# One addition into interleaved chunks of z, and more column levels tied behind the joins, in a four-layer convolution kernel

## The chip, the cores and the metric

The kernel runs on one core of a Trainium2 chip. The metric is the device time of one execution in microseconds (us). Times below are medians of several runs, or come from one profiled execution where that is said. The engines are named as in the profile: PE (matrix products; PEld is its weight load), DVE (VectorE), ACT (ScalarE), POOL (GpSimd), and SP, which issues most of the transfers (DMA). SBUF is the on-chip memory the engines work in; PSUM is the memory PE writes its products to.

## The reference

Four layers act in turn on x of 4 images x 64 channels x 256 x 256 pixels, in float32. Layers 0, 1 and 3 convolve every channel with a separable filter (made by a small sine network), which the kernel does as two products with Toeplitz matrices per channel, and add a multiple of the input. Layer 2 is the one that the change touches. It transforms each image to Haar coefficients in both directions, mixes the channels at every coefficient in two ways, shrinks and sums the two, and transforms back:

```python
f1 = haar2d(x)
acc = jnp.zeros_like(f1[:, :conv_w.shape[1]])
for i in range(v.shape[0]):          # two terms
    f3 = f1 * v[i]
    f4 = jnp.einsum('bchw,oc->bohw', f3, conv_w[i])
    f5 = jnp.sign(f4) * jax.nn.relu(jnp.abs(f4) - tau[i])
    acc = acc + f5
y = haar2d(acc, inverse=True)
return y + x
```

## The kernel before

The four images go through three kinds of stage. `convolutions(b)` does layers 0 and 1 and the forward Haar transform of image b, channel by channel, and stores coefficients in DRAM. `mixing(b)` does the channel mixing and the shrinking, in 64 groups g of four coefficient rows (two stored rows, 2g and 2g+1). `inverse(b)` does the inverse Haar transform and layer 3, channel by channel, for 64 channels. The convolutions of image b+1 run beside the mixing of image b, and their last part beside its inverse. Of images 0 to 2 some channels skip layer 3 at first (`put_off`), are stored (`late`), and are done in `convolution` beside the mixing of image 3.

The order of the work is written as events: each step has a time in ticks (`at`, `PLACE`), and the events are emitted in that order. The framework's planner then places the instructions on each engine's queue when the kernel is built; it may take an instruction ahead of its written tick, as long as its inputs and its explicit ties allow. What counts is the order in the trace.

The tile z (32,768 floats in each of 128 partitions) holds the mixed coefficients of one image. Its free dimensions before are n, s, x, c: n is the chunk (channels 16n to 16n+15), s the slot of a stored row (`slot(i)`, 128 of them), x the four pieces of a row, c the channel in the chunk.

In mixing, for each group: `mix` makes the products on PE; `scaled` (DVE, L502) and `scaled_too` (ACT, L507) multiply them by coefficients into f4, of 16 pieces of 64 channels. `N_ACT` says how many of the 16 pieces ACT takes: 12 for images 0 to 2, 8 for image 3. So DVE takes 4 pieces in one instruction, and for image 3 it takes 8 in two. `size` and `sign` are on ACT (L511, L514), `shrink` and `signed` on DVE (L518, L522). `add` (L528) sums the two terms into z, one DVE instruction for each of the group's two rows, 256 elements each. The output channels come in the order of the columns of `wmix`, n then c, and `add` writes them in runs of 16.

The column direction of the inverse transform is done on z itself. `level(n, chunk, begin, count)` does one step of it for one chunk of 16 channels: `halve` subtracts (L326) and then forms the other half by `scalar_tensor_tensor` (L329), in place, over n rows (or `count` of them) of 64 contiguous elements. Chunk 0 is not done in this way: its 16 channels go through PE instead (`halves`, `cols`). For chunks 1 to 3 there are levels n = 1, 2, 4, 8 and 16 in one piece each, n = 32 in two pieces of 16 rows and n = 64 in four. `butterfly` does a first small step for all chunks. A level of n rows needs the rows that the first 2n slots bring, so it may run while mixing still goes on.

In inverse, `fetch` (ACT, L569) copies one channel out of z, 512 elements that lie 64 floats apart for s and 16 for x; `rows` transforms them on PE; `join` (DVE, L598, L601, L602) adds the rest and makes u, from which layer 3 starts on PE (`contract`, L286 and L287; a copy on ACT, L300; the sum on DVE, L317). Channel c is fetched at tick `start + c + 0.414`, so chunk 1 is first wanted at tick 16, chunk 2 at 32 and chunk 3 at 48 of the stage.

`LATE[b]` lists pieces (chunk, n, i) of the levels that are held back: each is cut into two halves of 8 rows, placed at the two ticks given, and tied behind the join emitted last before it (`stay=True`, `behind[0]`, "not ahead of the joins"). Pieces that are not in the list are not tied.

Of the kernel before, what the change touches and what calls it, by code (L numbers as in the profile page):

```python
# [9 lines left out]
F32 = mybir.dt.float32  # L10
F32R = mybir.dt.float32r
AF = mybir.ActivationFunctionType
ALU = mybir.AluOpType
# [3 lines left out]
B, C, S, EMB, ORD = 4, 64, 256, 33, 64  # L17
P = 128
# [63 lines left out]
    "l add": 3.47,  # L82
}

LATE = (
    {
        (2, 64, 3): (21, 23),
        (3, 32, 0): (18, 19),
        (3, 32, 1): (25, 27),
# [2 lines left out]
        (3, 64, 2): (34, 35),  # L92
        (3, 64, 3): (37, 38),
    },
    {(2, 64, 3): (21, 23), (3, 64, 1): (24, 26), (3, 64, 2): (28, 31), (3, 64, 3): (34, 37)},
    {(2, 64, 3): (21, 23), (3, 64, 1): (24, 26), (3, 64, 2): (28, 31), (3, 64, 3): (34, 37)},
    {},
)

# [11 lines left out]
def conv_seq_kernel(ctx, tc, x, fz, fw, bias, decay, haar, haar_row, factors, vt, taut, wmix, out):  # L111
# [14 lines left out]
    nc = tc.nc  # L126
# [5 lines left out]
    zpool = ctx.enter_context(tc.tile_pool(name="zpool", bufs=1))  # L132
# [13 lines left out]
    bsb = const.tile([P, 3, C], F32, name="bsb")  # L146


    z = zpool.tile([P, 4, P, 4, 16], F32, name="z")

    sd = zpool.tile([P, 8, 2, 2, P], F32, name="sd")
    sums = zpool.tile([P, 4, 2, P], F32, name="sums")
# [6 lines left out]

    room = z.rearrange("p n s x c -> p (n s x c)")
    free = [0]

    def part(n, parts=P):
# [158 lines left out]
    def halve(even, odd, stay=False):  # L324

        first = nc.vector.tensor_sub(odd, even, odd)  # L326
        if stay and behind[0] is not None:
            tc.add_manual_dep(first.ins, behind[0].ins.name, order, reason="not ahead of the joins")
        nc.vector.scalar_tensor_tensor(even, even, 2.0, odd, ALU.mult, ALU.subtract)  # L329

    def level(n, chunk, begin=0, count=None, stay=False):

        count = n if count is None else count
        v = z.rearrange("p n s x c -> p n s (x c)")[:, chunk].rearrange("p (j e s) x -> p j e s x", e=2, s=P // 2 // n)
        halve(v[:, begin : begin + count, 0, 0, :], v[:, begin : begin + count, 1, 0, :], stay)

    def butterfly():

        v = z.rearrange("p n s (k h) c -> p n s k h c", k=2)
        for h in range(2):  # L340
            halve(v[:, :, 0, 0, h, :], v[:, :, 0, 1, h, :])

# [3 lines left out]
    def at(time, run, unit):  # L348
        events.append((time, len(events), run, unit))
# [104 lines left out]
    def mixing(b, start, n_act):  # L454

        st = {}

        def load(g):
            f = mx.tile([P, 2, S], F32, name=f"f_{b}_{g}", tag="f", bufs=3)
            nc.sync.dma_start(f, coef[b].rearrange("k c p w -> (k c) p w")[:, 2 * g : 2 * g + 2])  # L460
            st[g] = {"f": f}
            if g % GT == 0:
                t = mx.tile([P, 2, GT, 16], F32, name=f"vt_{b}_{g}", tag="vt")
                nc.sync.dma_start(t, scales[:, g // GT])
                st["vt", g // GT] = t

        def scale(g, i):
            return st["vt", g // GT][:, i, g % GT, :]

        def over(g, i, n):  # L470
            return scale(g, i)[:, :n].unsqueeze(2).to_broadcast([P, n, C])

        def mix(g):
            f = st[g]["f"]
            ps = psx.tile([P, 2, 2, S], F32, name=f"px_{b}_{g}", tag="mix")
            for q in range(2):
                for h in range(2):
                    for r in range(2):
                        half = slice(r * C, (r + 1) * C)
                        nc.tensor.matmul(  # L480
                            ps[:, r, q, h * P : (h + 1) * P],
                            f[half, q, h * P : (h + 1) * P],
                            wb[half],
                            start=True,
                            stop=True,
                        )
            if g == 0:

                one, two = ps[:, 0, 0], ps[:, 1, 0]
                d = mx.tile([P, S], F32, name=f"d_{b}", tag="mag")  # L490
                nc.vector.tensor_copy(d, two)
                nc.vector.tensor_sub(two, one, d)
                nc.vector.tensor_add(one, one, d)
            st[g]["f4"] = mx.tile([P, 16, C], F32, name=f"f4_{b}_{g}", tag="f4")
            st[g]["px"] = ps.rearrange("p r q (h i o) -> p r q (h i) o", h=2, i=2)

        def scaled(g):
            px, n = st[g]["px"], 16 - n_act
            for r in range(n // 4):
                j = slice(4 * r, 4 * r + 4)  # L500
                v = scale(g, 0)[:, j].unsqueeze(2).to_broadcast([P, 4, C])
                nc.vector.tensor_tensor(st[g]["f4"][:, j], px[:, r, 0], v, ALU.mult)  # L502

        def scaled_too(g, half):
            px, f4 = st[g]["px"], st[g]["f4"]
            for j in range(16 - n_act + half * (n_act // 2), 16 - (1 - half) * (n_act - n_act // 2)):
                nc.scalar.mul(f4[:, j], px[:, j // 4 % 2, j // 8, j % 4], scale(g, 0)[:, j : j + 1])  # L507

        def size(g):
            mag = st[g]["mag"] = mx.tile([P, 16, C], F32, name=f"mag_{b}_{g}", tag="mag")  # L510
            nc.scalar.activation(mag, st[g]["f4"], AF.Abs)  # L511

        def sign(g):
            nc.scalar.activation(st[g]["f4"], st[g]["f4"], AF.Sign)  # L514

        def shrink(g):
            mag = st[g]["mag"]
            nc.vector.tensor_sub(mag, mag, over(g, 1, 16))  # L518

        def signed(g):  # L520
            mag = st[g]["mag"]
            nc.vector.scalar_tensor_tensor(mag, mag, 0.0, st[g]["f4"], ALU.max, ALU.mult)  # L522

        def add(g):
            parts = st.pop(g)["mag"].rearrange("p (q x i) (n c) -> p q i x n c", q=2, i=2, n=4)
            for q in range(2):
                to = slot(2 * g + q)
                nc.vector.tensor_add(  # L528
                    z[:, :, to].rearrange("p n x c -> p x n c"), parts[:, q, 0], parts[:, q, 1]
                )  # L530


        for g in range(S // 4):
            for name, stage in zip(
                ("mix load", "mix", "scaled", "scaled too", "scaled rest", "size", "sign", "shrink", "signed", "add"),
                (
                    load,
                    mix,
                    scaled,
                    lambda g: scaled_too(g, 0),  # L540
                    lambda g: scaled_too(g, 1),
                    size,
                    sign,
                    shrink,
                    signed,
                    add,
                ),
            ):
                at(start + g + PLACE[name if b + 1 < B else "l " + name], stage, g)

    def inverse(b, start, put_off):

        st = {}
# [11 lines left out]

        def fetch(c):
            a = mx.tile([P, 2, 2, P], F32, name=f"zc_{b}_{c}", tag="mag")
            v = z[:, c // 16, :, :, c % 16].rearrange("p i (k h) -> p h k i", k=2)
            nc.scalar.copy(a, v)  # L569
            st[c]["z"] = a  # L570

# [38 lines left out]
        def when(tick, n, chunk, *span, stay=False):  # L610
            at(tick + PLACE["level"], lambda _: level(n, chunk, *span, stay=stay), 0)

        at(along + 11 + PLACE["level"], lambda _: butterfly(), 0)
        for chunk in range(1, 4):
            turn = start + 16 * (chunk - 1)
            for n in (1, 2, 4, 8):
                when(along + 12 + 3 * chunk if b + 1 < B else turn, n, chunk)
            if chunk == 3 and b + 1 < B:
                turn = start + 15
            when(turn + 1, 16, chunk)  # L620
            for n in (32, 64):
                for i in range(n // 16):
                    tick = LATE[b].get((chunk, n, i))
                    if tick is None:
                        when(turn + n // 16 + (n == 64) * 2 + 2 * i, n, chunk, 16 * i, 16)
                    else:
                        for j in range(2):
                            when(start + tick[j], n, chunk, 16 * i + 8 * j, 8, stay=True)

        for c in range(C):  # L630
            for name, stage in zip(("sooner", "early", "fetch", "rows"), (sooner, early, fetch, rows)):
                at(start + c + PLACE[name], stage, c)
            turn = start + c
# [75 lines left out]
    start = ready + 3  # L709
    for b in range(B):  # L710
# [10 lines left out]
        start = max(end + C, ready + 3)  # L721
# [5 lines left out]
def slot(i):  # L727

    if i == 0:
        return 0  # L730
    n = 1 << i.bit_length() - 1
    return (2 * (i - n) + 1) * (P // 2 // n)
# [104 lines left out]
```

## Time and profile before

| what | value |
|---|---|
| median of 3 runs | 2844.78 us (2844.46 to 2845.08) |
| the profiled execution, in the same measure | 2842.56 us |
| its span in the profile | 2840.7 us |
| PE busy | 2732.7 us, 96% |
| DVE busy | 2494.6 us, 88% |
| ACT busy | 2077.6 us, 73% |
| POOL busy | 333.9 us, 12% |
| first to last start of `add` (L528), image 0 | 448.7 to 846.9 us |
| the same, images 1, 2, 3 | 1051.8 to 1483.4, 1694.8 to 2126.4, 2332.5 to 2607.7 us |
| first to last start of `fetch` (L569), image 0 | 848.0 to 1029.6 us |
| the same, images 1 and 3 | 1483.8 to 1672.7, 2608.3 to 2823.8 us |
| granted PE clock | full speed throughout |

The span is what the profile records from its first to its last event; the time of the execution has 1.9 us around it. Busy time is the time in which at least one instruction of the engine was under way. Instructions of one engine overlap a little: the mean duration of one is somewhat longer than the distance from its start to the start of the next. A tick is no fixed time: in image 0, the 64 channels of the inverse take 182 us, about 2.9 us each.

### The profile page before, as it was taken

To read this page: it belongs to the slowest core of one execution; us is meant where nothing else is said; L and a number is where in the kernel's file an instruction comes from. 1 tells how busy PE (TensorE), PEld (TensorE's weight loads), DVE (VectorE), ACT (ScalarE), POOL (GpSimd) and SP (SyncE) were. 2 spreads that over 40 slices of the span, in tenths; PEclk is the share of its full clock that TensorE was granted. 3 is DMA by queue.
4 is the path that set the end of the run, shared out by engine and by line. 5 is a ranking of instruction groups with operands and counts; after the bars stand their busy time and mean duration, and the time that the engine had idled before them with its cause. 6 is when DMAs were issued, how large, how long until landed. Compare 5 with 4: busy or idle time off the path is not lost. (4 is left out here: it accounts for less than half of the span.)

```text
span 2840.7 us, 56683 instructions
## 1 busy us (share of the span) xinstructions
PE 2732.7 (96%) x18642; PEld 2438.6 (86%) x18642; DVE 2494.6 (88%) x4333; ACT 2077.6 (73%) x4941; POOL 333.9 (12%) x644
## 2 busy tenths in 40 slices
PE   9999999999999999999999999999999999899999
PEld 8999998888889898888889998888889987787998
DVE  5655558999998979999998879999998889999985
ACT  2333348999986559989886658999985669998554
POOL 0111111121111001212210001312210000000000
PEclk9999999999999999999999999999999999999999
DMA  6877787676667886777677986777778988787786
GB/s 200 258 232 231 227 239 220 209 208 208 206 207 251 287 257 203 211 212 209 205 216 246 292 262 201 210 210 214 208 212 241 296 277 249 234 253 228 227 240 200
DMA packets 597209, 653.20 MB, mean 230 GB/s; under 512 B 44625, under 2 KB 513204, under 8 KB 596660
## 3 DMA queue, kind: packets, MB, share of 16 engines
q1 hardware_dynamic: 545460, 599.82, 70.6%
q10 hardware_dynamic: 51456, 49.75, 5.1%
q8 instruction: 150, 2.46, 0.4%
q14 instruction: 143, 1.17, 0.1%
HBM read 428.34 MB, written 221.05 MB: 229 GB/s over the span
## 5 line engine op out<-in xcount | busy, mean ns | idle before, releaser
L286 PE MATMUL py<-t,a 128*128 128x256 f32 x3072 | 946.3, 390 | 48.7 <-ACT a L300 47.7
L300 ACT COPY a<-pa 128x512 f32<-128x512 f32 x768 | 475.1, 619 | 476.6 <-PE pa L287 448.3
L507 ACT ACTIVATE f<-px,vt 128x64 f32<-128x64 f32 x2816 | 607.6, 354 | 104.2 <-DVE f L502 101.9
L287 PEld LDWEIGHTS py<-t,a 128*128 128x128 f32 x3072 | 583.4, 190 | 79.3
L287 PE MATMUL py<-t,a 128*128 128x128 f32 x3072 | 590.0, 274 | 0.0
L286 PEld LDWEIGHTS py<-t,a 128*128 128x128 f32 x3072 | 479.4, 191 | 112.2 <-ACT a L300 74.6
L380 POOL TENSOR_TENSOR sd<-less 128x128 f32<-128x128 f32 (+4 forms) x320 | 188.5, 589 | 1829.7 <-DVE less L379 1498.1
L286 PE MATMUL pa<-t,y 128*128 128x256 f32 x1024 | 316.5, 391 | 45.0 <-DVE y L317 44.2
L569 ACT COPY zc<-z 128x512 f32<-128x512 f32 x256 | 280.8, 1105 | 104.6 <-PE pw L577 96.7
L518 DVE TENSOR_TENSOR mag<-mag,vt 128x1024 f32<-128x1024 f32 x256 | 316.5, 1236 | 7.5 <-ACT mag L511 6.7
L522 DVE SCALAR_TENSOR_TENSOR mag<-mag,f 128x1024 f32<-128x1024 f32 x256 | 317.4, 1240 | 0.9 <-ACT f L514 0.5
L286 PE MATMUL pa<-t,x 128*128 128x256 f32 x1024 | 308.7, 383 | 0.6 <-DMA pad<-z 0.6
L403 DVE TENSOR_TENSOR sp<-sd,sp 128x512 fp32r<-128x512 f32 x256 | 179.3, 700 | 145.7 <-ACT sp L398 144.3
L480 PE MATMUL px<-wb,f 64*128 64x128 f32 x4096 | 303.7, 285 | 2.2 <-ACT f L507 2.2
L511 ACT ACTIVATE mag<-f 128x1024 f32<-128x1024 f32 x256 | 293.9, 1148 | 5.2 <-DVE z L528 1.2
L514 ACT ACTIVATE f<-f 128x1024 f32<-128x1024 f32 x256 | 283.9, 1109 | 4.1
L480 PEld LDWEIGHTS px<-wb,f 64*128 64x128 f32 x4096 | 252.2, 187 | 36.5 <-ACT f L507 3.0
L317 DVE SCALAR_TENSOR_TENSOR y<-x,bsb,py 128x512 f32<-128x512 f32 x256 | 190.3, 743 | 44.0 <-PE py L287 40.6
L286 PE MATMUL pa<-t,u 128*128 128x256 f32 x748 | 224.6, 382 | 0.7 <-PE pw L577 0.7
L287 PEld LDWEIGHTS pa<-t,y 128*128 128x128 f32 x1024 | 194.5, 190 | 26.4
L287 PEld LDWEIGHTS pa<-t,x 128*128 128x128 f32 x1024 | 194.6, 190 | 26.3
L286 PEld LDWEIGHTS pa<-t,y 128*128 128x128 f32 x1024 | 155.6, 191 | 65.3 <-DVE y L317 62.8
(71 smaller groups left out, 4434.6 us busy)
## 6 DMA issues: line engine op xcount, KB each, us to landing
t<-pad SPq DMA_DIRECT2D x767, 256.0 KB, 4.1
x<-in_x SPq DMA_DIRECT2D x256, 256.0 KB, 3.9
coef<-co SPq DMA_DIRECT2D x256, 256.0 KB, 3.2
f<-coef SPq DMA_DIRECT2D x256, 256.0 KB, 3.5
r<-keep SPq DMA_DIRECT2D x256, 256.0 KB, 4.1
out_y<-y ACTq DMA_DIRECT2D x187, 256.0 KB, 4.2
keep<-sums SPq DMA_DIRECT2D x256, 128.0 KB, 2.8
keep<-sd SPq DMA_DIRECT2D x256, 128.0 KB, 2.7
```

The costliest lines, as they stand in the source:

```text
L286: nc.tensor.matmul(ps[:, m, :], src[:, 0, m * P : (m + 1) * P], t[:, ::-1], start=True, stop=False)
L287: nc.tensor.matmul(ps[:, m, P:], src[:, 1, m * P : (m + 1) * P], t[:, : P - 1 : -1], start=False, stop=True)
L300: nc.scalar.copy(a, s["p" + new])
L317: nc.vector.scalar_tensor_tensor(y, s[res], bsb[:, layer, c : c + 1], s["p" + new], ALU.mult, ALU.add)
L380: engine.tensor_tensor(t[:, :, :, half:length], v[..., 0], v[..., 1], ALU.subtract)
L480: nc.tensor.matmul(ps[:, r, q, h * P : (h + 1) * P], f[half, q, h * P : (h + 1) * P], wb[half], start=True, stop=True,)
L507: nc.scalar.mul(f4[:, j], px[:, j // 4 % 2, j // 8, j % 4], scale(g, 0)[:, j : j + 1])
L511: nc.scalar.activation(mag, st[g]["f4"], AF.Abs)
L514: nc.scalar.activation(st[g]["f4"], st[g]["f4"], AF.Sign)
L518: nc.vector.tensor_sub(mag, mag, over(g, 1, 16))
L522: nc.vector.scalar_tensor_tensor(mag, mag, 0.0, st[g]["f4"], ALU.max, ALU.mult)
L569: nc.scalar.copy(a, v)
```

## The change

Four things are altered together.

1. z is laid out as s, x, c, n: the chunk is now the innermost dimension. The columns of `wmix` are put in the order c, n to match. `add` then writes both rows of a group with one instruction of 512 elements, contiguous in runs of 256. `level` and `fetch` pick one chunk out by its innermost index, so the 64 elements of a row that a level reads and writes lie 4 floats apart, and the elements of a fetch 256 floats apart for s and 4 x 16 for x. `butterfly` now runs over 64 contiguous elements.
2. `scaled` for image 3 does its 8 pieces in one instruction instead of two.
3. More pieces are held back: two more for image 0, four more for images 1 and 2, and some of the ticks differ. Image 3 has none, as before.
4. For images 0 to 2 the levels of chunk 2 are written from tick 3 of the inverse on instead of 16.

```diff
+LATER = {
+    (2, 64, 1): (10, 12),
+    (2, 64, 2): (14, 16),
+    (2, 64, 3): (18, 20),
+    (3, 64, 0): (22, 23),
+    (3, 64, 1): (25, 26),
+    (3, 32, 1): (28, 29),
+    (3, 64, 2): (32, 34),
+    (3, 64, 3): (37, 40),
+}
+
 LATE = (
     {
+        (2, 64, 1): (10, 12),
+        (2, 64, 2): (14, 16),
         (2, 64, 3): (21, 23),
...
-    {(2, 64, 3): (21, 23), (3, 64, 1): (24, 26), (3, 64, 2): (28, 31), (3, 64, 3): (34, 37)},
-    {(2, 64, 3): (21, 23), (3, 64, 1): (24, 26), (3, 64, 2): (28, 31), (3, 64, 3): (34, 37)},
+    LATER,
+    LATER,
     {},
 )
...
-    z = zpool.tile([P, 4, P, 4, 16], F32, name="z")
+    z = zpool.tile([P, P, 4, 16, 4], F32, name="z")
...
-        v = z.rearrange("p n s x c -> p n s (x c)")[:, chunk].rearrange("p (j e s) x -> p j e s x", e=2, s=P // 2 // n)
+        v = z.rearrange("p s x c n -> p s (x c) n")[:, :, :, chunk]
+        v = v.rearrange("p (j e s) x -> p j e s x", e=2, s=P // 2 // n)
         halve(v[:, begin : begin + count, 0, 0, :], v[:, begin : begin + count, 1, 0, :], stay)
...
-        v = z.rearrange("p n s (k h) c -> p n s k h c", k=2)
+        v = z[:, 0].rearrange("p (k h) c n -> p k h (c n)", k=2)
         for h in range(2):
-            halve(v[:, :, 0, 0, h, :], v[:, :, 0, 1, h, :])
+            halve(v[:, 0, h], v[:, 1, h])
...
-            for r in range(n // 4):
-                j = slice(4 * r, 4 * r + 4)
-                v = scale(g, 0)[:, j].unsqueeze(2).to_broadcast([P, 4, C])
-                nc.vector.tensor_tensor(st[g]["f4"][:, j], px[:, r, 0], v, ALU.mult)
+            if n == 4:
+                nc.vector.tensor_tensor(st[g]["f4"][:, :4], px[:, 0, 0], over(g, 0, 4), ALU.mult)
+            else:
+                f4 = st[g]["f4"][:, :8].rearrange("p (r j) o -> p r j o", r=2)
+                v = scale(g, 0)[:, :8].rearrange("p (r j) -> p r j", r=2).unsqueeze(3).to_broadcast([P, 2, 4, C])
+                nc.vector.tensor_tensor(f4, px[:, :, 0], v, ALU.mult)
...
-            parts = st.pop(g)["mag"].rearrange("p (q x i) (n c) -> p q i x n c", q=2, i=2, n=4)
-            for q in range(2):
-                to = slot(2 * g + q)
-                nc.vector.tensor_add(
-                    z[:, :, to].rearrange("p n x c -> p x n c"), parts[:, q, 0], parts[:, q, 1]
-                )
+            parts = st.pop(g)["mag"].rearrange("p (q x i) o -> p q x i o", q=2, i=2)
+            to, step = slot(2 * g), slot(2 * g + 1) - slot(2 * g)
+            v = z.rearrange("p s x c n -> p s x (c n)")[:, to : to + step + 1 : step]
+            nc.vector.tensor_add(v, parts[:, :, :, 0], parts[:, :, :, 1])
...
-            v = z[:, c // 16, :, :, c % 16].rearrange("p i (k h) -> p h k i", k=2)
+            v = z[:, :, :, c % 16, c // 16].rearrange("p i (k h) -> p h k i", k=2)
             nc.scalar.copy(a, v)
...
-            if chunk == 3 and b + 1 < B:
-                turn = start + 15
+            if chunk > 1 and b + 1 < B:
+                turn = start + (3 if chunk == 2 else 15)
             when(turn + 1, 16, chunk)
...
-        "wmix": lay(g["L2_conv_conv_w"].transpose(2, 0, 1).reshape(C, 2 * C)),
+        "wmix": lay(g["L2_conv_conv_w"].transpose(2, 0, 1).reshape(C, 2, 4, 16).swapaxes(2, 3).reshape(C, 2 * C)),
```

More of the change, by code (lines that the diff above doesn't have):

```diff
@@ L158, in conv_seq_kernel @@
     late = dram.tile([B, C, P, 2, S], F32, name="late")
-    room = z.rearrange("p n s x c -> p (n s x c)")
+    room = z.rearrange("p s x c n -> p (s x c n)")
     free = [0]
```

## The prediction

> **What bounds the kernel now.** The page says PE 96%, DVE 88%, ACT 73% over the span, but that is an average over stages. So I read the busy times by stage first. Columns: stretch in us; its length; then PE, weight loads, DVE, ACT and POOL busy us with their instruction counts; granted clock; DMA share; GB/s.
>
> ```profile
> core 0: us, PE busy (x) PEld busy (x) DVE busy (x) ACT busy (x) POOL busy (x), PEclk, DMA share, GB/s
> 450.00:848.00 398.00, 371.57 (x2658) 323.04 (x2657) 394.05 (x660) 374.95 (x1070) 77.46 (x120) 1.00 0.69 207
> 1052.00:1495.00 443.00, 422.32 (x2968) 369.73 (x2967) 434.58 (x721) 394.36 (x1099) 91.50 (x140) 1.00 0.71 210
> 2333.00:2600.00 267.00, 242.48 (x1952) 210.82 (x1951) 266.32 (x446) 257.45 (x672) 0.00 (x0) 1.00 0.82 247
> ...
> 880.00:980.00 100.00, 98.30 (x635) 89.05 (x634) 94.47 (x186) 64.80 (x86) 2.59 (x10) 1.00 0.87 276
> 1530.00:1625.00 95.00, 94.16 (x611) 85.82 (x610) 83.65 (x163) 60.01 (x80) 2.59 (x10) 1.00 0.89 285
> 2168.00:2265.00 97.00, 95.42 (x617) 86.89 (x617) 86.12 (x169) 62.02 (x83) 2.58 (x10) 1.00 0.89 282
> 2608.00:2745.00 137.00, 136.27 (x886) 125.92 (x887) 134.45 (x220) 73.27 (x95) 0.00 (x0) 1.00 0.77 227
> ```
>
> The first three rows are mixing of images 0, 1 and 3 (image 2 repeats image 1's): DVE is idle 4.0 of 398, 8.4 of 443, 0.7 of 267 us, while PE lacks 20 to 27 us in each. There every microsecond of DVE is a microsecond of time. The last four rows are stretches of the inverse stages: PE lacks only 1 to 2 us, but DVE has little left: 5.5, 11.4, 10.9 and 2.5 us. So DVE work is the currency of this change, at full price in mixing and in image 3's inverse, and above a small reserve elsewhere.
>
> Second, the groups by shape (count; then busy us, mean ns of one), for prices:
>
> ```profile
> L514 ACT ACTIVATE f<-f 128x1024 f32<-128x1024 f32 x256 | 283.9, 1109 | 4.1
> L569 ACT COPY zc<-z 128x512 f32<-128x512 f32 x256 | 280.8, 1105 | 104.6 <-PE pw L577 96.7 <-DVE z L528 2.3
> L398 ACT CAST sp<-sd 128x512 fp32r<-128x512 f32 x256 | 178.3, 696 | 4.2 <-POOL sd L380 4.2
> L326 DVE TENSOR_TENSOR z<-z 128x1024 f32<-128x1024 f32 x69 | 84.2, 1225 | 0.3
> L329 DVE SCALAR_TENSOR_TENSOR z<-z 128x512 f32<-128x512 f32 x42 | 28.7, 687 | 0.0
> ```
>
> The reader should see that L569, which reads z with a large step between elements, needs 1105 ns for 512 elements, as long as the contiguous L514 for 1024, where contiguous 512 cost 696 (L398).
>
> Third, the order of DVE in time (start, length):
>
> ```profile
> 1302.61 0.75 DVE L528 TENSOR_TENSOR z<-mag 128x256 f32<-128x256 f32 x2
> 1303.28 0.74 DVE L317 SCALAR_TENSOR_TENSOR y<-x,bsb,py 128x512 f32<-128x512 f32 x1
> ...
> 1305.07 1.22 DVE L326 TENSOR_TENSOR z<-z 128x1024 f32<-128x1024 f32 x1
> 1306.21 0.74 DVE L317 SCALAR_TENSOR_TENSOR y<-y,bsb,py 128x512 f32<-128x512 f32 x1
> ...
> 1597.63 0.68 DVE L326 TENSOR_TENSOR z<-z 128x512 f32<-128x512 f32 x1
> 1598.23 0.42 DVE L601 TENSOR_TENSOR u<-t 128x256 f32<-128x256 f32 x1
> ```
>
> From start to start: the two adds of a group take 0.67 us, a 1024-element level 1.14, a 512-element one 0.60. And levels of image 1 stand at 1305 us, though its inverse begins at 1484 (first fetch): the untied ones were moved forward into mixing, where DVE is full.
>
> **Part 1, one add instead of two.** 0.67 becomes one 512-element instruction, 0.60 by the row at 1597.63. 64 groups give 64 x 0.07 = 4.5 us per image, in mixing, on DVE's path. Writes become contiguous; the old 16-element runs cost no more than contiguous rows of 256 (L601 0.42), so nothing more is gained.
>
> **Part 2, merged scaled, image 3 only.** Two L502 take 0.67 from start to start; 512-element rows that read PSUM take 0.60 (L598, at 2664.56) to 0.66 (L317, at 1303.28). I take 0.63: 64 x 0.04 = 2.4 us (bounds 0.6 to 4.5). [...]
>
> **Part 3, levels tied.** A piece is one 1024-element sub and one such scalar_tensor_tensor, 2.27 us. Each image has 3 chunks x 7 = 21. Tied before: 7, 4, 4, 0 for images 0 to 3 (so 14 + 17 + 17 + 21 = 69 untied, L326's count). After: 9, 8, 8, 0. Mixing sheds 2 x 2.27 = 4.5 us for image 0, 4 x 2.27 = 9.1 for images 1 and 2. In the inverse stages they return as halves, 2 x 2 x 0.60 = 2.4 us a piece, behind joins. What queues behind a tied half is the next join's t and u, and PE's next a3 waits for u. The earlier written turn of chunk 2 costs nothing: its untied levels stood in mixing anyway. The last tied pieces (ticks 18 to 20 for chunk 2, 40 for chunk 3) lie 8 ticks or more ahead of the fetches at 32 and 48; at some 2.9 us a tick (64 fetches from 848.0 to 1029.6) that is 23 us of room.
>
> **Part 4, the level's new step.** With the chunk index innermost, one chunk's 64 values lie 4 floats, 16 bytes, apart, in both inputs and the output of every level. No DVE row before has such a step (the widest is 2 floats, L366, at the contiguous 0.42). Bounds: nothing, from L366; and the L569 row's extra. There a stepped element costs (1105 - 696)/512 = 0.80 ns more, and the contiguous slope on ACT is (1109 - 696)/512 = 0.81: two turns per element instead of one. DVE's slope is (1225 - 689)/512 = 1.05 ns. I take the upper end, one turn more, because L569 is the only row with a step past 2 floats; its step is 64 floats, so the lower end stays possible. Then a 1024 level costs 1.14 + 1.07 = 2.21, a half 0.60 + 0.54 = 1.14.
>
> [...]
>
> Elements per image: 3 x (64 + 128 + 256 + 512 + 7 x 1024) = 24,384, twice (sub and the other), x 1.05 ns = 51.1 us.
>
> Fetch (ACT) goes from a step of 64 to 256 floats: bounds zero and another turn, 256 x 0.4 us; I take zero, since it is stepped already; it runs in the inverse, where ACT is busy 64.8 of 100 us, and without that room it would be 26 us per image. Butterfly, weights and the count of DMAs: zero, same elements.
>
> **The sum**, in us of time:
> - Mixing 0: -4.5 (add) - 4.5 (moved) + 12 remaining pieces x 2.14 = 25.7, + small levels 2,880 x 2 x 1.05 ns = 6.0: +22.7.
> - Mixing 1 and 2: -4.5 - 9.1 + 13 x 2.14 (27.9) + 6.0 = +20.3 each, 40.6.
> - Inverse 0: halves 14 x 1.2 = 16.8 become 18 x 2 x 1.14 = 40.9: +24.1 against 5.5 idle: +18.6.
> - Inverse 1 and 2: 9.6 become 16 x 2.27 = 36.4: +26.8 against 11.1: +15.7 each, 31.3. PE is full after these stretches, so it can't win this back. Bounds for the three overflows together: 0 (all cover in the late ticks used) to 78 (no cover).
> - Mixing 3: -4.5 - 2.4 = -6.9.
> - Image 3's levels, all untied: 51.1 - 2.5 = +48.6.
>
> Together +154.9. The profiled execution took 2842.56 (span 2840.7), so 2997.5; the median of the runs lies 2.2 higher: **3000 us**. Its own range, by the overflow's bounds, is 2950 to 3030.
>
> **Rivals.**
> *The step is free on DVE* (faster). For it: L366's step of 2 floats is free, and 4 floats lie nearer to it than L569's 64. Against: L569. Price: mixing -9.0, -13.6, -13.6, -6.9; the moved pieces 4.8 + 9.6 + 9.6 = 24 us come back under idle 27.7, with perhaps 8 lost to late joins: -35, so 2810 (2801 to 2826). It decides below about 0.2 ns per element, where part 4 no longer pays for parts 1 to 3. Chance 0.22.
>
> *The extra is a time, not a turn*: 0.80 ns per element, 39.0 us per image. The same sum: 15.3 + 2 x 12.3 + 14 + 2 x 11.7 + 36.5 - 6.9 = 107, 2952. For it: the extra may be the memory's own time; against: it equals ACT's slope so exactly. 0.20.
>
> *Reads and write pay each*: twice the extra, another 204 us, 3204. Against: contiguous in-place levels run at one slope with three streams. 0.07.
>
> *The change doesn't do what it says*: tied levels still land in mixing, because a tie only says "not ahead of" one join. Before, the tied ones of image 1 stand at 1570 to 1615, inside the inverse, so I give it 0.04; price 9 us per image, 27 on top of my case. My forecast has the remaining 0.47.
>
> **Numbers.** The free step holds 0.22 of the chance, so the range must reach into it: 2805 to 3050. Telling from no change needs about 0.2%, 6 us. Faster 0.22; slower 0.76; within 0.2%, 0.02, for an extra near the deciding 0.2 ns.
>
> **What would show it.** L326 of 128x1024: 1225 ns if free, 2040 for the timed extra, 2300 for a turn, over 3000 for both. L528 must show 256 instructions near 0.69 us, L326 59 of 1024 elements and 62 of 512. Mixing 1 should last some 20 us longer with DVE still full, and DVE waits before PE's a3 and y3 should appear in 2608 to 2800. If L326 is at 1225 ns, my prediction falls at part 4; if it is at 2300 and the time is under 2950, the inverse stages' overflow was hidden.

## The result, and the profile after

| what | before | after |
|---|---|---|
| median | 2844.63 us (2844.46 to 2845.08, 4 runs) | 2980.54 us (2978.04 to 2981.92, 4 runs) |
| the profiled execution, and its span | 2842.56, 2840.7 us | 2980.06, 2978.2 us |
| DVE busy | 2494.6 us | 2627.6 us |
| PE busy | 2732.7 us, 96% | 2770.5 us, 93% |
| ACT busy | 2077.6 us | 2085.2 us |
| mean granted PE clock | 1.0 | 0.998 |

The kernel is slower: the ratio is 1.0476, with a 95% interval of 1.0464 to 1.0489. That is 135.9 us between the medians, 137.5 between the profiled executions. DVE did 133 us more work, PE only 38 more, and PE's share fell.

To find where the time went, both traces are cut at the same events: the first `add` of an image opens its mixing stage, its first `fetch` opens its inverse stage. Lengths in us:

| | mixing 0 | inverse 0 | mixing 1 | inverse 1 | mixing 2 | inverse 2 | mixing 3 | inverse 3 |
|---|---|---|---|---|---|---|---|---|
| before | 399.3 | 203.8 | 432.0 | 211.0 | 432.1 | 205.6 | 275.8 | 232.4 |
| after | 417.3 | 222.2 | 452.1 | 223.6 | 452.1 | 216.9 | 288.7 | 256.2 |
| difference | +18.0 | +18.4 | +20.1 | +12.6 | +20.0 | +11.3 | +12.9 | +23.8 |
| predicted | +22.7 | +18.6 | +20.3 | +15.7 | +20.3 | +15.7 | -6.9 | +48.6 |

The differences add up to 137.1 us. The busy times of some of these stages in the changed kernel, with the columns named in the first line:

```profile
core 0: us, PE busy (x) PEld busy (x) DVE busy (x) ACT busy (x) POOL busy (x), PEclk, DMA share, GB/s
449.10:866.40 417.30, 376.76 (x2660) 325.12 (x2661) 412.81 (x598) 376.19 (x1069) 80.33 (x120) 0.99 0.66 197
1088.60:1540.70 452.10, 416.45 (x2903) 361.22 (x2902) 438.30 (x637) 389.52 (x1090) 94.40 (x140) 1.00 0.67 200
2433.30:2722.00 288.70, 249.50 (x2000) 216.77 (x1998) 288.46 (x352) 266.43 (x687) 0.00 (x0) 1.00 0.78 234
2722.00:2978.20 256.20, 235.71 (x1496) 212.13 (x1496) 208.67 (x311) 118.27 (x148) 0.00 (x0) 1.00 0.66 200
```

Look at the columns of DVE and PE. In mixing 1, DVE is idle 13.8 of 452.1 us, PE 35.7. In mixing 3 DVE is idle 0.2 us: it is as full as before, although the merged adds and `scaled` took work out of that stage. In image 3's inverse PE, which the prediction's row 2608 to 2745 had full, now lacks 20.5 us of the whole stage. In the kernel before it lacked 4.6:

```profile
2608.30:2840.70 232.40, 227.80 (x1496) 211.49 (x1494) 192.70 (x328) 117.16 (x147) 0.00 (x0) 1.00 0.74 220
```

The groups by shape in the changed kernel (count; busy us, mean ns of one; idle us before, with what ended it), and one of the kernel before:

```profile
L583 ACT COPY zc<-z 128x512 f32<-128x512 f32 x256 | 282.4, 1117 | 90.0 <-PE pw L591 76.3 <-DVE y L330 6.8 <-DVE z L544 1.8
L544 DVE TENSOR_TENSOR z<-mag 128x512 f32<-128x512 f32 x256 | 177.5, 693 | 1.2
L339 DVE TENSOR_TENSOR z<-z 128x1024 f32<-128x1024 f32 x59 | 122.7, 2086 | 0.4
L339 DVE TENSOR_TENSOR z<-z 128x512 f32<-128x512 f32 x62 | 69.1, 1118 | 0.0
```

```profile
L326 DVE TENSOR_TENSOR z<-z 128x512 f32<-128x512 f32 x42 | 28.6, 686 | 0.0
```

The changed program's L339 is the old L326, L544 the old L528, L583 the old L569. A level of 1024 elements went from 1225 to 2086 ns and one of 512 from 686 to 1118: (2086 - 1225)/1024 and (1118 - 686)/512 are both 0.84 ns per element. A mean duration is a little more than what the queue pays (2086 ns for 1.96 us from start to start), so the order of DVE in time is the better price (start, length):

```profile
2589.35 0.67 DVE L518 TENSOR_TENSOR f<-px,vt 128x512 f32<-128x512 f32 x1
2589.95 1.20 DVE L534 TENSOR_TENSOR mag<-mag,vt 128x1024 f32<-128x1024 f32 x1
2591.08 0.67 DVE L544 TENSOR_TENSOR z<-mag 128x512 f32<-128x512 f32 x1
2591.69 1.20 DVE L538 SCALAR_TENSOR_TENSOR mag<-mag,f 128x1024 f32<-128x1024 f32 x1
...
2726.01 2.06 DVE L342 SCALAR_TENSOR_TENSOR z<-z 128x1024 f32<-128x1024 f32 x1
2727.95 0.71 DVE L598 TENSOR_TENSOR w<-pw,w 128x512 fp32r<-128x512 f32 x1
```

From start to start the merged `scaled` (L518) takes 0.60 us, the merged `add` (L544) 0.61, and a stepped 1024-element level 1.94. The median distance from a level's start to the next start on DVE is 1.96 us against 1.14 before, and for 512 elements 1.01 against 0.60: 0.80 ns per element. An image has 2 x 24,384 elements of levels, so the four cost DVE 195,072 x 0.80 = 156 us more. The two merges were built as described and have the durations foreseen.

### The profile page after: what moved, and what is told of

Same layout as the page of the kernel before. It is cut to its first block, busy times and chain, and to the rows that moved or that the text cites. A ratio compares the mean times of both kernels' runs of the same rounds, so it can differ in the third digit from the quotient of the medians.

```text
span 2978.2 us, 56292 instructions
## 1 busy us (share of the span) xinstructions
PE 2770.5 (93%) x18642; PEld 2445.3 (82%) x18642; DVE 2627.6 (88%) x4033; ACT 2085.2 (70%) x4941; POOL 338.9 (11%) x644
## 3 DMA queue, kind: packets, MB, share of 16 engines
q14 instruction: 139, 1.14, 0.1%
## 5 line engine op out<-in xcount | busy, mean ns | idle before, releaser
L583 ACT COPY zc<-z 128x512 f32<-128x512 f32 x256 | 282.4, 1117 | 90.0 <-PE pw L591 76.3
L534 DVE TENSOR_TENSOR mag<-mag,vt 128x1024 f32<-128x1024 f32 x256 | 313.5, 1225 | 7.6 <-ACT mag L527 7.3
L300 PEld LDWEIGHTS pa<-t,y 128*128 128x128 f32 x1024 | 195.7, 191 | 26.8
```

What stands on the lines that cost most here:

```text
L300: nc.tensor.matmul(ps[:, m, P:], src[:, 1, m * P : (m + 1) * P], t[:, : P - 1 : -1], start=False, stop=True)
```

## The experiments

Twelve kernels ran. "Levels" are the instructions of `halve` called from `level`. "Ties" are the new lists of held-back pieces with the earlier turn of chunk 2.

### What a step costs: one look at single instructions

`p_steps` runs single kinds of 512-element instruction, six times each, with different steps (in floats) on different operands.

```diff
+        nc.vector.tensor_tensor(flat3, flat, flat2, ALU.add)
+        nc.vector.tensor_tensor(flat3, stepped(2), flat2, ALU.add)
+        nc.vector.tensor_tensor(flat3, stepped(3), flat2, ALU.add)
+        nc.vector.tensor_tensor(flat3, stepped(4), flat2, ALU.add)
...
+        nc.vector.tensor_tensor(stepped(4), flat, flat2, ALU.add)
...
+        nc.vector.tensor_tensor(stepped(4, 512, 4096), stepped(4), stepped(4, 512, 4096), ALU.subtract)
...
+        nc.scalar.copy(flat3, flat)
...
+        nc.scalar.copy(flat3, stepped(4))
```

> No part of the reference: 512-element DVE additions and ACT copies with contiguous operands and with operands stepped by 2, 3, 4, 8 and 64 floats, six of each. Expected on DVE: contiguous 690 ns, steps 2 and 3 the same. With step 4, theory A (paid once per element, whatever the operands): about 1118 ns with one stepped operand as with three. Theory B (paid by each stepped operand): some 830 ns with one, 1118 with three. [...] On ACT: contiguous about 690, step 64 about 1105; step 4 about 1105 if the edge is the same for both engines.

Its groups by shape. L29 is contiguous; L30, L31, L32 and L34 have one input at steps 2, 3, 4 and 64; L37 has only the output at step 4; L39 has all three operands at step 4, in place. L42 and L45 are ACT's copy, contiguous and from step 4.

```profile
L29 DVE TENSOR_TENSOR d<-d 128x512 f32<-128x512 f32 x6 | 4.2, 692 | 6.2 <-ACT d L46 6.1
L30 DVE TENSOR_TENSOR d<-a,d 128x512 f32<-128x512 f32 x6 | 4.2, 692 | 7.9 <-ACT a L48 7.8
L31 DVE TENSOR_TENSOR d<-a,d 128x512 f32<-128x512 f32 x6 | 5.0, 835 | 0.2
L32 DVE TENSOR_TENSOR d<-a,d 128x512 f32<-128x512 f32 x6 | 6.4, 1061 | 0.2
L34 DVE TENSOR_TENSOR d<-a,d 128x512 f32<-128x512 f32 x6 | 6.1, 1023 | 0.2
L37 DVE TENSOR_TENSOR a<-d 128x512 f32<-128x512 f32 x6 | 6.5, 1078 | 0.2
L39 DVE TENSOR_TENSOR a<-a 128x512 f32<-128x512 f32 x6 | 6.6, 1096 | 0.2
L42 ACT COPY d<-d 128x512 f32<-128x512 f32 x6 | 3.7, 618 | 74.1 <-DVE d L36 74.1
L45 ACT COPY d<-a 128x512 f32<-128x512 f32 x6 | 6.8, 1136 | 0.2
```

Step 2 is free (692), step 3 is paid in part (835), step 4 in full (1061), and 64 costs no more than 4 (1023). One stepped operand and three cost nearly the same (1061 to 1096): the step is paid once per element, 0.72 to 0.79 ns. So what the levels pay is the step itself.

### Which part of the change costs: layout alone, ties alone

`e1_layout` is the changed kernel with the old ties; `e2_ties` is the kernel before with the new ones.

```diff
 # e1_layout, against the kernel after
-    LATER,
-    LATER,
+    {(2, 64, 3): (21, 23), (3, 64, 1): (24, 26), (3, 64, 2): (28, 31), (3, 64, 3): (34, 37)},
+    {(2, 64, 3): (21, 23), (3, 64, 1): (24, 26), (3, 64, 2): (28, 31), (3, 64, 3): (34, 37)},
...
-            if chunk > 1 and b + 1 < B:
-                turn = start + (3 if chunk == 2 else 15)
+            if chunk == 3 and b + 1 < B:
+                turn = start + 15
```

> The changed kernel with the old list of tied pieces and the old turn of chunk 2: layout, single add and merged scaled alone. Theory (DVE time: a stepped element costs 0.84 ns more, read from the level groups of the changed kernel, 2086 ns against 1225): the untied pieces fall back into mixing, where DVE is full. Mixing 0: 14 pieces x 2 x 0.86 + 4.8 - 4.5 = +24; mixing 1 and 2: 17 x 1.72 + 4.8 - 4.5 = +29.5 each; inverse 0: 14 halves x 2 x 0.43 = 12 against 5.5 idle = +6.5, inverse 1 and 2 nothing; image 3 +36.7 as in the changed kernel. Together +126, and some 10 to 20 more for waits behind long levels: 2970 to 2990, so within 0.5% of the changed kernel. Rival (the ties are what slows): near 2845, below 2900.

Measured: 2981.46 us (2979.36 to 2982.48), ratio 1.048 (1.0464 to 1.0495). The layout is the whole loss; the ties on top of it are worth 0.9 us, which is less than the spread. By stages the ties do act: with them mixing 0, 1 and 2 are 2.8, 8.1 and 8.8 us shorter, and the three inverse stages behind them 5.6, 8.0 and 7.4 us longer.

```diff
 # e2_ties, against the kernel before
+    (2, 64, 1): (10, 12),
+    (2, 64, 2): (14, 16),
...
+    LATER,
+    LATER,
...
-            if chunk == 3 and b + 1 < B:
-                turn = start + 15
+            if chunk > 1 and b + 1 < B:
+                turn = start + (3 if chunk == 2 else 15)
```

> The kernel before with only the new list of tied pieces and the new turn of chunk 2; layout, adds and scaled as before. Theory: mixing sheds 4.5 + 9.1 + 9.1 = 22.7 us, and the inverse stages take back 4.8 + 9.6 + 9.6 us of DVE work under 27.7 us of idle DVE, at most 8 lost: 2822 to 2830, faster than before. Rival (tied halves cost the joins what mixing wins): 2840 to 2850. Rival (the ties are the slow part): above 2900.

Measured: 2848.03 us (2845.72 to 2850.36), ratio 1.0012 (1.0002 to 1.0021). A miss. The ties did what they say: mixing 1 lost 6.6 us of DVE work (426.3 to 419.7). But it became only 0.9 us shorter (432.0 to 431.1), and each inverse stage of images 0 to 2 became 1.3 to 2.4 us longer. This was the first sign that "DVE full" and "DVE bounds" are not the same.

### Is it DVE's time? The same extra work without the step

`e3_longer` keeps the contiguous layout and both small adds, with the new ties. Behind each half of a level it puts a further DVE instruction in place, of about the length that the step adds (768 elements behind a 1024-element half).

```diff
+        rows = {1: (0, 0), 2: (1, 1), 4: (2, 2), 8: (5, 6), 16: (12, 12)}[even.shape[1]] if longer else (0, 0)
+        if rows[0]:
+            t = odd[:, : rows[0]]
+            nc.vector.tensor_tensor(t, t, t, ALU.max)
         nc.vector.scalar_tensor_tensor(even, even, 2.0, odd, ALU.mult, ALU.subtract)
+        if rows[1]:
+            t = even[:, : rows[1]]
+            nc.vector.tensor_tensor(t, t, t, ALU.max)
```

> The kernel before with the new ties, and after each half of a level one more DVE instruction in place on part of the same contiguous rows (element by element the larger of a value and itself), sized so that each level takes about as long as the stepped one: 768 elements after 1024, 320 or 384 after 512, 128 after 256, 64 after 128. z is contiguous as before. Theory (only the DVE time of the levels matters): each mixing and inverse stage lengthens as in the changed kernel, plus 4.5 us per image for the adds that stay double and some for the extra instructions: 2985 to 3020. Rival (something else of the layout slows: the fetch with a larger step, other engines held off by stepped access): clearly less, 2870 to 2940.

Measured: 2940.12 us (2937.3 to 2943.49), ratio 1.0336 (1.032 to 1.0351), with DVE busy 2646.2 us, more than the changed kernel's 2627.6. That is below the range expected. So 95 us come from DVE time alone, whatever uses it, but 40 are missing. The levels also stood elsewhere: the planner sees the extra instructions and put fewer levels into mixing 0 and 1 (18,304 and 27,520 elements, against 28,544 and 30,592 in the changed kernel, which has the same ties). Of a step's price it seems not to know: `e1_layout` has 38,784 elements in mixing 1, as many as the kernel before. Two explanations for the 40 us were open, the plan and the step itself.

### Were the levels filling time that mixing had anyway?

`e4_no_levels` is the kernel before without the levels n = 16, 32 and 64, so that the transform of 48 channels stays incomplete.

```diff
-            when(turn + 1, 16, chunk)
-            for n in (32, 64):
+            for n in ():
                 for i in range(n // 16):
```

> The kernel before without the levels n = 16, 32 and 64 of chunks 1 to 3; the transform of 48 channels is left incomplete, all else is done. It asks whether DVE's time is the time of mixing. Theory of the prediction (every microsecond of DVE in mixing is one of time): mixing 0, 399.3 us before, loses some 14 x 2.27 = 32; mixing 1 and 2, 432 us, lose 17 x 2.27 = 39 each; image 3 loses 48 in mixing and inverse together: 2690. Rival (the untied levels fill gaps of DVE that another chain leaves; only work added above them costs): mixing 0 to 2 lose at most 10 each, image 3's inverse some 10 to 25 until PE binds: 2800 to 2835.

Measured: 2824.08 us in a single execution, beside 2845.04 for the kernel before: 21 us less, for 161 us less of DVE work (2494.6 to 2333.7). Mixing 1 without these levels, and then the same stage of the kernel before (stretch; length; PE, weight loads, DVE, ACT, POOL busy; clock, DMA, GB/s):

```profile
1050.60:1476.10 425.50, 411.08 (x2903) 359.58 (x2902) 395.74 (x677) 389.69 (x1090) 74.00 (x140) 1.00 0.71 212
```

```profile
1051.80:1483.80 432.00, 411.32 (x2901) 359.68 (x2901) 426.32 (x709) 388.20 (x1090) 91.50 (x140) 1.00 0.70 209
```

DVE lost 30.6 us of work and the stage 6.5 us of time. PE is busy the same 411 us in both. The stage has a length of about 425 us that DVE does not set, and the levels filled what DVE had left of it. DVE was full because the planner had filled it. The opposite test, work added in the same order, is `q_layout_blind` below.

### The same plan for each: held queues

These kernels are built twice. The first build gives the order of each engine's instructions; the second is tied to that order, instruction behind instruction. All have the old ties, two small adds per group and the two unmerged `scaled`, so only the levels differ.

```diff
+STEPPED, LONGER, PLANNED = False, True, (False, False)
...
+        for queue in plan:
+            for i, j in zip(queue, queue[1:]):
+                tc.add_manual_dep(written[j], written[i].name, tie, reason="in the given order")
...
+    plan = build(*PLANNED)[1]
+    nc = build(STEPPED, LONGER, plan)[0]
```

`q_longer` is contiguous levels with the extra instructions, in the order planned for the kernel before. `q_layout` is stepped levels in the order that is planned when the extra instructions are known.

> z contiguous and the old ties, with the extra DVE instructions of e3_longer, but every engine's queue is held in the order of the kernel before, which was planned without them: the plan doesn't know of the longer levels, as the plan of the changed kernel doesn't know of the price of the step. Theory (the extra 40 us of the changed kernel against e3_longer come from a plan made with wrong durations): 2980 to 3010, about the changed kernel plus 18 for the adds that stay double. Rival (the layout has a further cost of its own, such as the fetch or the other engines): about 2940, as e3_longer.

Measured: 2999.0 us (2997.51 to 3000.2), ratio 1.054 (1.052 to 1.0561), DVE busy 2662.1. With a plan that doesn't know of it, extra DVE work without any step, and with the old fetch, costs all that the change costs, and 18 us more. Its mixing 1:

```profile
1091.90:1556.20 464.30, 420.43 (x2902) 365.25 (x2901) 459.58 (x759) 389.46 (x1091) 93.95 (x140) 0.99 0.66 195
```

DVE has 33.3 us more work there than in the kernel before, and the stage is 32.3 us longer.

```diff
-STEPPED, LONGER, PLANNED = False, True, (False, False)
+STEPPED, LONGER, PLANNED = True, False, (False, True)
```

> The interleaved layout with its stepped levels, the adds double and scaled unmerged, old ties, but the queues are held in the order planned for contiguous levels with the extra DVE instructions, so the plan knows about how long a level takes. Theory (wrong plan): 2935 to 2965, 20 to 45 us faster than the changed kernel although its adds are double. Rival (a further cost of the layout): 2985 to 3005.

Measured: 2981.08 us (2980.6 to 2981.81), ratio 1.0478 (1.0457 to 1.0499). A plan that knows the price does not help the stepped levels. That the planner's ignorance makes the change slow falls with this run.

`q_layout_blind` is stepped levels in the order planned for the kernel before: against `q_layout` only the plan differs. Against `e1_layout` it lacks the merged adds and `scaled`, and the order is another.

```diff
-STEPPED, LONGER, PLANNED = True, False, (False, True)
+STEPPED, LONGER, PLANNED = True, False, (False, False)
```

> The same instructions as q_layout (interleaved layout, adds double, scaled unmerged, old ties), held in the order of the kernel before, planned for contiguous levels without extra work. With q_layout it gives the worth of a plan that knows of the longer levels, at the same layout. Theory (DVE time alone, wrong plan): as q_longer, 2999, within 10. Then the better plan is worth some 18 us (2981). Rival (order doesn't matter for stepped levels): 2981 within 3.

Measured: 2981.06 us (2978.58 to 2982.41), ratio 1.0479 (1.0463 to 1.0495). Its DVE is busy 2646.0 us, `e1_layout`'s 2624.7: the two merges save 21.3 us of DVE, about the 18.0 + 2.4 of the prediction, and 2981.06 against 2981.46 says that in all this is worth nothing in time. As the orders differ, the stages say more. Mixing 1 and 2 hold 38,784 elements of levels in both; there `e1_layout` has 5.3 and 5.1 us less DVE work and is 2.0 and 2.2 us shorter. Image 3's two stages, where `e1_layout` has 14,720 elements in mixing and `q_layout_blind` 5,632, are 3.8 us longer in `e1_layout`. The mixing 1 of `q_layout_blind`:

```profile
1087.00:1549.30 462.30, 418.28 (x2903) 362.92 (x2902) 457.32 (x709) 389.46 (x1091) 99.61 (x140) 0.99 0.66 195
```

In the same order as before, DVE went from 426.3 to 457.3 us, +31.0, and the stage from 432.0 to 462.3, +30.3. So the stage answers differently by direction: 31 us off DVE bought 6.5, 31 on DVE cost 30.

In this one order the step is not dearer than separate instructions: `q_longer` took 2999.0 us with 16.1 us more DVE work than `q_layout_blind`.

### A credit by itself

`g_scaled` is the kernel before with the merged `scaled` alone, in five rounds.

```diff
-            for r in range(n // 4):
-                j = slice(4 * r, 4 * r + 4)
...
+                f4 = st[g]["f4"][:, :8].rearrange("p (r j) o -> p r j o", r=2)
...
+                nc.vector.tensor_tensor(f4, px[:, :, 0], v, ALU.mult)
```

> The kernel before with the merged scaled of image 3 alone. In the changed kernel the merged instruction stands 0.60 us from its start to the next, where two took 0.67. Theory: DVE is without a gap through image 3's mixing even with no levels (274.1 of 274.8 us in e4_no_levels), so 64 x 0.07 = 4.5 us less DVE is up to 4.5 us less time: 2840 to 2843. Rival (ACT or PE takes over at once): 2844 to 2846.

Measured: 2849.32 us (2847.7 to 2851.14), ratio 1.0018 (1.0009 to 1.0027). A miss. Its mixing 3:

```profile
2334.30:2614.90 280.60, 251.32 (x2002) 218.37 (x2000) 279.84 (x413) 265.35 (x687) 0.00 (x0) 0.99 0.81 241
```

DVE is full again (279.84 of 280.60 us), and the stage is 4.8 us longer than before, though its `scaled` got cheaper: levels of 12,928 elements now stand in it instead of 5,632. The planner filled the room that was made. In the changed kernel 14,720 stand there, which fits the +12.9 where -6.9 was predicted.

### Is it the length of one piece?

A stepped 1024-element instruction holds DVE's queue 1.96 us. `f_halves` cuts all such pieces of the changed kernel in two.

```diff
-            when(turn + 1, 16, chunk)
+            for j in range(2):
+                when(turn + 1, 16, chunk, 8 * j, 8)
...
-                        when(turn + n // 16 + (n == 64) * 2 + 2 * i, n, chunk, 16 * i, 16)
+                        for j in range(2):
+                            when(turn + n // 16 + (n == 64) * 2 + 2 * i, n, chunk, 16 * i + 8 * j, 8)
```

> The changed kernel with every level of 1024 elements cut in two of 512, so that no level holds DVE for more than 1.1 us; DVE gets 118 x 0.07 = 8 us of work more. Theory (the long hold of 2.1 us keeps joins and sums waiting and so costs time beyond the work): below 2975. Rival (only the work counts): 2981 to 2990.

Measured: 2982.71 us (2980.62 to 2984.16), ratio 1.0486 (1.047 to 1.0502). DVE's work grew by 9.4 us (2627.6 to 2637.0). If shorter holds gain anything, it is no more than this work costs.

### The same plan, with the step and without

`q_longer_known` is contiguous levels with the extra instructions in its own plan, which is the order that `q_layout` was held to. `q_layout_ties` is stepped levels in the order of `e3_longer`, with its ties.

```diff
 # q_longer_known, against q_longer
-STEPPED, LONGER, PLANNED = False, True, (False, False)
+STEPPED, LONGER, PLANNED = False, True, None
...
-    plan = build(*PLANNED)[1]
+    plan = build(*PLANNED)[1] if PLANNED else None
...
 # q_layout_ties, against q_layout
...
-    {(2, 64, 3): (21, 23), (3, 64, 1): (24, 26), (3, 64, 2): (28, 31), (3, 64, 3): (34, 37)},
-    {(2, 64, 3): (21, 23), (3, 64, 1): (24, 26), (3, 64, 2): (28, 31), (3, 64, 3): (34, 37)},
+    LATER,
+    LATER,
...
-            if chunk == 3 and b + 1 < B:
-                turn = start + 15
+            if chunk > 1 and b + 1 < B:
+                turn = start + (3 if chunk == 2 else 15)
```

> Contiguous z, old ties, with the extra DVE instructions, in the plan that knows of them: the very order that q_layout used (2981). e3_longer, the same with the new ties, took 2940. Theory (the new ties together with a plan that knows are what won the 40 us): about 2980. Rival (at the same order and the same DVE work, stepped levels cost time of their own): about 2940.

Measured: 2934.4 us (2933.96 to 2935.64), ratio 1.0317 (1.0296 to 1.0337), DVE busy 2645.3. `q_layout`, with DVE busy 2646.6 in the same order, took 2981.08.

> The interleaved layout with stepped levels and double adds, held in the exact order of e3_longer, new ties included. Theory (ties and plan): 2935 to 2955, as e3_longer, which would make it some 30 faster than the changed kernel. Rival (stepped levels cost time of their own): 2975 to 2985.

Measured: 2974.26 us (2974.19 to 2977.12), ratio 1.0459 (1.0438 to 1.048); `e3_longer` in the same order took 2940.12.

So in these two orders the step costs 47 and 34 us more than the same DVE time in separate instructions. The 47 are spread over all stages, with the most in mixing 1 and 2 (10.8 and 9.7 us). In mixing 1 DVE's work is nearly the same, 435.8 and 434.4 us, but DVE is idle 12.0 us in `q_layout` and 2.6 in `q_longer_known`. **What makes this difference is not settled.** Three things differ, and no run isolates them:
- An extra instruction can stand back: in `q_longer_known`, taken in order, at least one other DVE instruction comes between a 512- or 1024-element half and its extra in all but 2 of 222 cases, and four or more in 90. A stepped level of 1024 elements holds the queue for its 1.96 us. But `f_halves` gained nothing, in another plan.
- The mean granted PE clock of `q_layout` is 0.993, of `q_longer_known` 0.999. Over 2979 us that is an estimated 18 us, if PE held up the time throughout.
- In image 3's inverse other DVE instructions last longer beside stepped levels: `y` from `u` 771 ns for 745, `t` from `pw` 719 for 684. The `u` of `join` in `q_layout`, and then in `q_longer_known`, within that stage alone:

```profile
L623 DVE TENSOR_TENSOR u<-t 128x256 f32<-128x256 f32 x64 | 28.8, 450 | 1.0
```

```profile
L623 DVE TENSOR_TENSOR u<-t 128x256 f32<-128x256 f32 x64 | 27.0, 421 | 0.6
```

But from the start of `u` to that of the next instruction, where DVE does not wait, it is 0.34 us in both (0.335 for those of `q_layout` that last 0.5 us or more), so DVE's queue loses nothing by it. Only what waits for `u` can be late, by 0.03 us on average. That stage is 5.9 us longer in `q_layout` (267.9 for 262.0).

No kernel that does the whole computation was faster than the kernel before.

## Why the prediction was right, and where it was wrong

The direction and the cause hold: the layout makes each level pay for its step on a DVE that has no room for it, and 2980.54 us lies within both ranges, 20 us below the point.

**The step (part 4): right in kind, too high in size.** The prediction took one more turn, 1.05 ns per element; the trace shows 0.80 from start to start. That was the price of its rival "a time, not a turn". L569's extra of 0.80 ns on ACT, the nearest row, was already that number; turning it into a turn by ACT's slope was the wrong inference. That the two numbers are the same is partly luck: against the 618 ns of ACT's own contiguous copy in `p_steps`, the extra of that row is (1105 - 618)/512 = 0.95. Paying per operand and a free step both fell, by L339 at 2086 ns for 1225 and by `p_steps` (at step 4 1061 ns with one stepped operand and 1096 with three, 692 contiguous).

**The sentence "every microsecond of DVE is a microsecond of time": the step that failed.** It came from DVE's idle time in mixing, 4.0, 8.4 and 0.7 us. It holds for work added in the same order (+31.0 for +30.3 in `q_layout_blind`, +33.3 for +32.3 in `q_longer`) and not for work taken away (-30.6 for -6.5 in `e4_no_levels`). Where the planner knew of the added work it did not hold either: in `q_longer_known` 151 us more DVE work, over the whole kernel, cost 90 us. And where the layout had first made the stage longer, taking work away paid in part: from `e1_layout` to the changed kernel mixing 1 lost 13.7 us of DVE work and 8.1 us of time. So the credits hardly came. The merges, 18.0 + 2.4 us: none in all in `q_layout_blind` against `e1_layout`. The ties, 22.7 us off mixing and part of it back in the inverse stages: -0.9 on the layout, +3.4 without it. `scaled` alone: +4.7. The idle share of an engine that the planner fills with work that could stand elsewhere says nothing of what the stage would need without it.

**The two errors cancelled in part.** With the measured 0.80 the same working gives 107 us, as its rival says: 2952. So the size of the step was 48 us too high. In these 107 the merges are a credit of 20.4 us. The ties are one of some 8, with what they bring back in the inverse stages: without them the working has 23.1 + 2 x 28.0 us in the three mixings and 6 in the three inverses, in place of 15.3 + 2 x 12.3 and 37.4. Without both credits it comes to 135 us; `q_layout_blind`, which has neither the new ties nor the merges, measured 136.6, and the changed kernel 136. The forecast lay only 20 us too high because 48 too many stood against 28 of credits that did not come. By stages even the 135 are partly luck: the working has 27.6, 32.5 and 32.5 us for mixing 0 to 2 and 6, 0 and 0 for their inverses, where `q_layout_blind` has 21.1, 30.1 and 31.1, and 14.2, 4.9 and 4.3.

**By stages.** Mixing 1 and 2 came within 0.3 us (+20.1 and +20.0 for +20.3), but by this cancelling: DVE's work in mixing 1 grew by 12.0 us, near the 12.3 that the working gives at 0.80, and the other 8 us are idle time of DVE (13.8 us for 5.7), which the forecast had as still full. Image 3's two stages together were +36.7 for +41.7; their split was wrong by 20 to 25 us, because levels moved forward into the room that mixing 3 was thought to gain.

**The overflow in the inverse stages.** It came: +18.4, +12.6 and +11.3 us for 18.6, 15.7 and 15.7. The first agrees by luck: DVE's work there grew by 18.2 us, not 24.1, and none of it was covered by idle time. In the other two it grew by 22.1 us each, not 26.8, and 9.5 and 10.8 were covered. Waits of PE's `pa` on DVE's `u` appeared in image 3's inverse as foreseen (6.7 us in its first 192, none before), but they are a part only; the first row of waits in mixing 1 is larger. The waits of PE there, in the changed kernel and then before (engine, tile, line waited for; us, times, longest):

```profile
PE pa L299 <- DVE y L330: 25.8, 30, 2.0
```

```profile
PE pa L286 <- DVE y L317: 14.4, 20, 1.6
```

The layers' sum `y` stands in DVE's queue behind the levels, and PE's next products wait for it.

**Fetch at zero: right.** 1117 ns for 1105, at a step of 256 instead of 64 floats. **The merges' own prices: right**, 0.61 and 0.60 us from start to start; only their worth was wrong. **The change does what it says: right**, L544 256 times, 59 levels of 1024 and 62 of 512.

## What to carry to other kernels

A layout that makes one instruction contiguous moves its step to whoever reads the data next: count the elements on each side, and price a step of 4 floats or more (in `p_steps` 1061 ns at 4 and 1023 at 64, for 692) at the extra of the nearest stepped row (here 0.80 ns per element on DVE, against 0.07 us saved per merged pair). Before calling an engine the bound because it is full, look for work on it that could stand elsewhere in time: take that work out, and see whether the stage gets shorter. Price gains and losses separately where a planner fills the gaps.

## What the runs showed of the hardware that was not expected

In `p_steps` the 512-element DVE addition took 692 ns with one operand at step 2, 835 at 3 and 1061 at 4, and the subtraction with all three at step 4 nearly the same (1096). ACT's copy from step 4 paid more than DVE: (1136 - 618)/512 = 1.01 ns per element, for DVE's 0.72 to 0.79.

PE's granted clock fell to one half four times in the changed kernel, behind pauses of 1.70 to 1.99 us. The order of PE in the changed kernel (start, length; in brackets the idle time before, and its releaser):

```profile
1320.04 0.60 PE L299 MATMUL py<-t,a 128*128 128x256 f32 x2
1320.48 0.39 PE L300 MATMUL py<-t,a 128*128 128x128 f32 x2
1322.85 1.06 PE L299 MATMUL pa<-t,y 128*128 128x256 f32 x2 [1.99 <-DVE y L330]
1323.71 0.64 PE L300 MATMUL pa<-t,y 128*128 128x128 f32 x2
```

After a pause of 1.99 us a pair of products of the same shape takes 1.06 us instead of 0.60. The granted clock of the 20 us from 1320 to 1340 is 0.91, so some 1.8 us are lost on top of the pause. The changed kernel has four such places, each 3.41 us at half clock, behind pauses of 1.70, 1.70, 1.99 and 1.99 us. It has 29 pauses of 1.5 us and more, and its two longest, 2.77 and 2.27 us, bring no such place. The kernel before has 6 such pauses, and no such place past its start.

So the length of the pause alone does not decide. The places begin 204.80, 662.19 and 675.84 us apart, which is 60, 194 and 198 times 3.4133 us. If the time is cut into windows of that length, the window ahead of each place holds 1.70, 1.70, 1.99 and 1.99 us of idle PE, while the two longest pauses are split by an edge: the windows on its two sides hold 1.46 and 1.68 us, and 0.73 and 1.54. In this trace both windows with 1.99 us of idle PE were followed by one at half clock, of the six with 1.70 to 1.88 us two were, and of those with less none. The idle time within one window thus tells these four places better than the length of a pause does, though not from 1.70 to 1.88 us.

Four places of 3.41 us at half clock are an estimated 7 us of the 137. `g_scaled` has a granted clock of 0.99 in the mixing 3 printed above, the kernel before 1.00 in its own; that may be part of the +4.7, which is argued and was not tried.
